# Four changes to the order of VectorE's work in the attention of a convolution block

## The chip, the cores and the metric

The kernel runs on one core of one Trainium2 chip. The metric is device time in microseconds from start to end of one execution, as the median of several runs. The profile is of one execution, taken by the hardware profiler. Engines are named as the profile names them: PE is TensorE, DVE is VectorE, ACT is ScalarE, POOL is GpSimd, SP is SyncE, which only issues transfers here.

## The reference

The input is x with 8 images of 512 channels and 32x32 pixels, all in fp32. The block normalises it in groups of 16 channels, runs a block of convolutions with attention on it, and adds x:

```python
t = cbs(x, cv1_w, cv1_bn, 0)                      # 1x1, 512 -> 512, batch norm, silu
ys = [t[:, :C], t[:, C:]]                         # C = 256
for i in range(N):                                # N = 2 bottlenecks
    yi = ys[-1]
    z = cbs(yi, m_cv1_w[i], m_cv1_bn[i], 1)       # 3x3, 256 -> 256
    z = bot_attention(z, m_qkv_w[i], m_rw[i], m_rh[i])
    z = jax.nn.silu(bn_eval(conv2d(z, m_cv2_w[i], 0), m_cv2_bn[i]))
    ys.append(yi + z)
return cbs(jnp.concatenate(ys, axis=1), cv2_w, cv2_bn, 0)   # 1x1, 1024 -> 512
```

The attention has 4 heads of 64 channels over the 1024 pixels:

```python
logits = jnp.einsum('bhdi,bhdj->bhij', q, k + r) * HD ** (-0.5)   # r = rw + rh
a = jax.nn.softmax(logits, axis=-1)
out = jnp.einsum('bhij,bhdj->bhdi', a, v)
```

The outermost step is `x + block(_gn(x))`.

## The kernel before

The images follow each other, and each goes through: 3x3 convolution of the first bottleneck (a Winograd form: `tiles_in` makes the inputs on VectorE, `conv3x3` multiplies, `columns_out` and `rows_out` put the outputs together), its projection to q, k and v, its attention, its 1x1 convolution `m2`, then the same for the second bottleneck, then the last 1x1 convolution. The first 1x1 convolution of the next image (`cv1`) lies at the end of the first bottleneck's attention, which is why the next image's group norm is computed during that attention.

The instructions of each engine run in the order in which they were put into that engine's queue. The order is set by hand with `tc.issue_after(ins)`: what is written under it gets its place behind `ins`. A tile from a pool with `bufs=n` waits until the tile that had the same place n allocations before has been read. The page's `L` numbers are lines of the kernel before.

**Projection.** Image 1 uses `project`, and images 2 to 8 use `project_strassen`, which multiplies 2x2 blocks with seven products instead of eight, and needs more sums on VectorE. Its last five operations finish the second half of the pixels (`half` 1) for the first 128 channels (`c` 0): k1 += u (L626), add_r(0, 1), which adds rw (L577) and rh (L578) to k1, v1 += u (L628) and q1 += u (L629). The sums for the second 128 channels' r are put off to `later()`.

**Attention** (`attention_fast`). There are four groups g: two blocks of 128 channels (two heads each) times two halves of 512 query pixels. A group has eight blocks j of 128 key pixels, taken in pairs. So an attention has 16 pairs, and i counts them. For each pair:

- `logits(pair)`: TensorE makes the logits of two heads by 512 queries for each j (L662, eight matmuls, which the trace shows as 16 records), in a PSUM tile `l_ps` of the pool `ps_big` (3 tiles of two banks). ScalarE takes Exp of it into `pt` (L666). VectorE adds the `pt` into `acc`: the first pair of a group by one sum of its two halves (L672), later pairs by two sums (L674).
- `times_v(previous pair)`: TensorE multiplies the previous pair's `pt` by v into `av_ps` (L688). There is one `av_ps` tile (`ps_av`, bufs=1), two banks, for a whole group. After the last pair of a group it is evicted: ScalarE copies the first bank to `ao` (L695), VectorE adds the second (L696). The next group's first product waits for that.

TensorE is therefore one pair ahead with logits: at a group change it does the new group's first two pairs of logits, the old group's sums of Exp, and then the new group's first product.

**Divisions.** `sums(g)` adds `acc` over partitions with matmuls (`s_ps`, L706). ScalarE copies the row, and it goes through DRAM to be spread over partitions, is inverted by `spread(g)` (L750), goes to DRAM again and comes back as `rs`, broadcast over the partitions. `scale(g, rs)` multiplies `ao` by it (L762). `spread(g - 1)` is placed at the third pair of group g, and `scale(g - 2)` at the first pair.

**Work behind attention.** `behind` maps a group, or a group and a pair, to a function that is called there. In the first bottleneck `ahead` is called in each of the four groups. It takes one step of the next image's group norm with `next(norm)`: statistics of two channel blocks (L443), statistics of the other two, the mean over groups of channels (a matmul `gm_ps`, L449, in a `ps_big` tile, and small sums on VectorE), then deviation and the normalising of x (L477). The first group takes none, groups 1, 2 and 3 take one each, and one more is taken in the third pair of group 2. In image 1, `ahead` also makes 3x3 weights for the second bottleneck (`make`, tiles `u_new`) on VectorE.

Of the kernel before, what the change touches and what calls it, by code (L numbers as in the profile page):

```python
# [47 lines left out]
ALU = mybir.AluOpType  # L48
# [13 lines left out]
def kernel(  # L62
# [16 lines left out]
    nc = tc.nc  # L79
# [33 lines left out]
    def load_w1():  # L113
        w = ring([P, NX, 2 * C], "w1")
        nc.sync.dma_start(w, cv1_w.rearrange("(k p) o -> p k o", p=P))
        return w
# [189 lines left out]
    def load_u(n, oc, i):  # L306
        u = new_u("u")
        nc.sync.dma_start(u, u_dram[n][oc][i])
        return u
# [7 lines left out]
    def img(ap):  # L317
        return ap.rearrange("p (h w) -> p h w", w=F)

    def inner(yp, c, half):  # L320
        return yp[:, c, 1 + half * ROWS : 1 + (half + 1) * ROWS, :].rearrange("p h w -> p (h w)")

    def stages(act, small, ps_big, ps_av, n_pt):
# [6 lines left out]
        def table_of(func):  # L330

            nc.scalar.activation(spare, zero, func)
# [204 lines left out]
        def project_strassen(n, z, sq, mid):  # L537
# [6 lines left out]
            tt = nc.vector.tensor_tensor  # L544
# [25 lines left out]
            def v_of(ap):  # L570
                return ap.rearrange("p (j o) -> p j o", o=P)

            def add_r(c, half, src=None):
                dst = img(kr[:, c, ts(half, HALF)])
                rw = rw_sb[:, n, c, :].unsqueeze(1).to_broadcast([P, ROWS, F])
                rh = rh_sb[:, n, c, ts(half, ROWS)].unsqueeze(2).to_broadcast([P, ROWS, F])
                tt(dst, dst if src is None else img(src), rw, ALU.add)  # L577
                tt(dst, dst, rh, ALU.add)  # L578

            t = act.tile([P, 4, HALF], F32, tag="pt", name="t_z", bufs=n_pt)  # L580
            t1, t2, t3, t4 = (t[:, i] for i in range(4))
# [40 lines left out]
            with tc.issue_after(freed.ins):  # L622
                tt(v3, v2, v_of(m5[:, 2]), ALU.add)
                last = tt(v2, v2, v_of(ps_v[:, 0]), ALU.subtract)
            with tc.issue_after(last.ins):
                tt(k1, k1, u[:, 1], ALU.add)  # L626
                add_r(0, 1)
                tt(v1, v1, v_of(u[:, 2]), ALU.add)  # L628
                tt(q1, q1, u[:, 0], ALU.add)  # L629

# [6 lines left out]
        def attention_fast(n, z, at, behind, sq=None, mid=None):  # L637
# [3 lines left out]
            q, kr, vT, later = (*project(n, z), None) if sq is None else project_strassen(n, z, sq, mid)  # L641
# [6 lines left out]
            pairs = [steps[i : i + PAIR] for i in range(0, len(steps), PAIR)]  # L648
            pts, accs, avs = {}, {}, {}

            def logits(pair):
                g, j0 = pair[0]
                c, half = groups[g]
                pt = act.tile([P, PAIR, 2, HALF], F32, tag="pt", name="pt", bufs=n_pt)
                pts[pair[0]] = pt
                for i, (_, j) in enumerate(pair):
                    ps = ps_big.tile([P, 2, HALF], F32, tag="big", name="l_ps")
                    for hd in range(2):
                        r = slice(hd * HD, (hd + 1) * HD)
                        for kh in range(2):  # L660
                            o = j * P + kh * HD
                            nc.tensor.matmul(  # L662
                                ps[kh * HD : (kh + 1) * HD, hd, :], kr[r, c, o : o + HD],
                                q[r, c, ts(half, HALF)], start=True, stop=True,
                            )
                    exp = nc.scalar.activation(pt[:, i], ps, AF.Exp, scale=SCALE)  # L666
                if pair is pairs[-1]:
                    with tc.issue_after(exp.ins):
                        table_of(AF.Silu)
                if j0 == 0:  # L670
                    accs[g] = act.tile([P, 2, HALF], F32, tag="acc", name="acc", bufs=2)
                    return nc.vector.tensor_tensor(accs[g], pt[:, 0], pt[:, 1], ALU.add)  # L672
                for i in range(PAIR):
                    ins = nc.vector.tensor_tensor(accs[g], accs[g], pt[:, i], ALU.add)  # L674
                return ins

            def times_v(pair):
                g, j0 = pair[0]
                c, half = groups[g]
                pt = pts.pop(pair[0])  # L680
                if j0 == 0:
                    avs[g] = ps_av.tile([P, 2, HALF], F32, tag="av", name="av_ps")
                for i, (_, j) in enumerate(pair):
                    for kh in range(2):
                        r = slice(kh * HD, (kh + 1) * HD)
                        for hd in range(2):
                            o = c * P + hd * HD
                            nc.tensor.matmul(  # L688
                                avs[g][hd * HD : (hd + 1) * HD, kh, :], vT[r, j, o : o + HD],
                                pt[r, i, hd, :], start=(j == 0), stop=(j == NJ - 1),  # L690
                            )
                if j0 + PAIR == NJ:
                    av = avs.pop(g)
                    dst = ao[:, c, ts(half, HALF)]
                    nc.scalar.copy(dst, av[:, 0])  # L695
                    nc.vector.tensor_tensor(dst, av[:, 1], dst, ALU.add)  # L696

            def sums(g):

# [46 lines left out]
            def spread(g, s_dram):  # L746

                rs = act.tile([P, HALF], F32, tag="rs", name="rs", bufs=2)
                rc = small.tile([P, QP], F32, tag="rc", name="rc", bufs=2)
                nc.vector.reciprocal(rc, total(g, s_dram))  # L750
                r_dram = tc.dram_tile([2, HALF], F32, name=f"r_dram{at + g}")
                nc.sync.dma_start(r_dram.rearrange("h (i r) -> (h i) r", r=QP), rc)
                for hd in range(2):
                    nc.sync.dma_start(
                        rs[hd * HD : (hd + 1) * HD, :], r_dram[hd : hd + 1, :].to_broadcast([HD, HALF])
                    )
                return rs

            def scale(g, rs):
                c, half = groups[g]  # L760
                dst = ao[:, c, ts(half, HALF)]
                nc.vector.tensor_tensor(dst, dst, rs, ALU.mult)  # L762
# [2 lines left out]


            NQ = NJ // PAIR
            s_drams, rss = {}, {}
            for i in range(len(pairs) + 1):
                if i < len(pairs):  # L770
                    added = logits(pairs[i])
                    g, at_q = divmod(i, NQ)
                    with tc.issue_after(added.ins):
                        if at_q == NQ - 2 and g > 0:
                            rss[g - 1] = spread(g - 1, s_drams[g - 1])
                        if i == 1 and later is not None:
                            later()
                        if at_q == 0 and g > 1:
                            scale(g - 2, rss.pop(g - 2))
                if i > 0:  # L780
                    g, j0 = pairs[i - 1][0]
                    if j0 == 0 and g > 0:
                        s_drams[g - 1] = sums(g - 1)
                    times_v(pairs[i - 1])
                    with tc.issue_after(added.ins):
                        behind.get(g if j0 == 0 else (g, j0 // PAIR), lambda: None)()
            with tc.issue_after(added.ins):
# [2 lines left out]
            g = len(groups) - 1  # L790
# [319 lines left out]
    with tc.issue_after(made.ins):  # L1110
# [4 lines left out]
        for at in bn_m1:  # L1115
            last = nc.vector.tensor_scalar(sh[:, at : at + NM], sh[:, at : at + NM], -1 / 12, None, ALU.mult)
# [5 lines left out]
    last = made  # L1122
# [6 lines left out]
    for b in range(B):  # L1129
# [41 lines left out]
        norm = s.group_norm(xs) if more else iter(())  # L1171
        groups = iter(range(NM * NH))

        def ahead():
            nonlocal w1
            g = next(groups)
            if g > 0:
                next(norm, None)
            if g == 0:
                w1 = load_w1() if more else load_w2(1)  # L1180
                if b > 0:
                    for at in ((0, 0), (0, 1), (0, 2), (1, 0)):
                        us[at] = load_u(1, *at)
            if b == 0:
                if g == 0:
                    raws[1, 1, 0], raws[1, 1, 1] = load_raws_y0(1, 1)
                    make(1, 1, [2])
                    del us[1, 2]
                elif g <= NM:
                    make(1, 1, [0], [g - 1])  # L1190
# [14 lines left out]

        NG = NM * NH
        behind = {g: ahead for g in range(NG)} | {NG: first, NG + 1: second}
        behind[NG - 2, 2] = lambda: next(norm, None)
        if b == 0:
            behind[-1] = lambda: make(1, 0, range(PAIRS))  # L1210
        ao, check = s.attention_fast(0, z, b * N * NM * NH, behind, sq.get(0), mid)
        last = s.m2(0, ao, y1, lambda oc, half: inner(y2, oc, half))
# [44 lines left out]
        behind = {1: ahead, NG: first, NG + 1: second}  # L1257
# [4 lines left out]
        last = s.m2(1, ao, y2, lambda oc, half: ylast[:, oc, ts(half, HALF)])  # L1262
# [27 lines left out]
    with tc.If(held < P):  # L1290
        with ExitStack() as gs:
# [6 lines left out]
            g = stages(g_act, g_small, g_big, g_av, 3)  # L1298
# [67 lines left out]
```

## Time and profile before

The median of three runs is 2366.81 us (2366.19 to 2371.23).

| what | before |
|---|---|
| span of the profiled execution | 2365.4 us |
| mean granted TensorE clock | 0.997 |
| VectorE, sums of Exp (L674 and L672) | 469.5 and 78.3 us |
| VectorE, division (L762) x64 | 44.1 us busy, 65.8 us idle before it |
| VectorE, eviction (L696) x64 | 43.8 us |
| TensorE, product with v (L688) and logits (L662) | 487.8 and 486.1 us |
| chain of waits, TensorE | 89% of the span |

A group's busy time is the union of its instructions' times; "idle before" is the time in which that engine stood still just ahead of such an instruction, with what ended it. The arrow in a timeline line, such as `[0.15 <-DVE ao L696]`, says the same for one instruction. In the timeline neighbours of the same kind are merged, and x16 counts them.

### The profile page before, as it was taken

The page shows a single profiled execution, that of the slowest core. Times are in us where ns is not written, and L with a number is a line of the kernel's source. Part 1 is how long each engine was busy: PE and PEld are TensorE (multiplying, and loading weights), DVE is VectorE, ACT ScalarE, POOL GpSimd, SP SyncE. Part 2 cuts the span into 40 slices and gives each one's busy share as a digit, 9 for nine tenths or more (in the row PEclk, how much of TensorE's full clock was granted, in tenths as well). Part 3 has the DMA queues.
Part 4 walks back from the last instruction along what each step waited for, and adds up shares of the span by engine and source line. Part 5 has one row for each costly group of instructions (what it writes and reads, how often), then busy time and mean ns, then how long its engine had stood idle before and what let it go on. Part 6 is the DMA issues. An engine that isn't in the chain of part 4 may idle for free.

```text
span 2365.4 us, 36291 instructions
## 1 busy us (share of the span) xinstructions
PE 2321.6 (98%) x14794; PEld 1181.0 (50%) x14794; DVE 1751.7 (74%) x2811; ACT 944.5 (40%) x1246; POOL 87.9 (4%) x305
## 2 busy tenths in 40 slices
PE   7999999999999999999999999999999999999998
PEld 4536346363553635536364463645536364463643
DVE  8866777677786877868678675886767867677674
ACT  1442524435244351544425344253433525335352
POOL 1000000000100001000010000100001000000001
PEclk9999999999999999999999999999999999999999
DMA  7412225030340304303052031611207021160202
GB/s 251 152 53 89 91 90 213 16 129 15 123 176 15 130 15 164 140 10 130 23 208 89 29 112 33 248 42 54 86 28 263 29 85 55 42 221 15 85 10 69
DMA packets 93069, 226.39 MB, mean 96 GB/s; under 512 B 27872, under 2 KB 49312, under 8 KB 80224
## 3 DMA queue, kind: packets, MB, share of 16 engines
q1 hardware_dynamic: 81376, 174.71, 21.8%
q0 software_dynamic: 11520, 49.29, 5.3%
q8 instruction: 118, 1.93, 0.3%
q14 instruction: 55, 0.45, 0.1%
HBM read 190.41 MB, written 33.55 MB: 95 GB/s over the span
## 4 chain that ended last, share of the span: by engine, by line
PE 89%; DVE 6%; DMA 2%; ACT 2%; issue 1%; SPq 0%; POOL 0%; DVEq 0%; ACTq 0%
PE av_ps L688 16%; PE l_ps L662 15%; PE c_ps L879 14%; PE ps L343 12%; PE c L934 8%; PE p_ps L556 7%; PE c_new L934 6%; PE m_ps L900 5%; PE pv_ps L560 3%; DVE acc L674 2%; ACT pt L666 1%; PE p_ps L560 1%; DVE acc L672 1%; PE s_ps L724 1%; DMA rs<-r_dram 1%; PE s_ps L706 1%
## 5 line engine op out<-in xcount | busy, mean ns | idle before, releaser
L666 ACT ACTIVATE pt<-l_ps 128x1024 f32<-128x1024 f32 x512 | 494.9, 1023 | 425.0 <-PE l_ps L662 423.6
L674 DVE TENSOR_TENSOR acc<-acc,pt 128x1024 f32<-128x1024 f32 x384 | 469.5, 1223 | 84.9 <-ACT pt L666 60.1
L688 PE MATMUL av_ps<-pt,vT 64*64 64x512 f32 x4096 | 487.8, 593 | 10.7 <-DVE ao L696 10.7
L662 PE MATMUL l_ps<-q,kr 64*64 64x512 f32 x4096 | 486.1, 591 | 0.9
L879 PEld LDWEIGHTS c_ps<-v_in,u 128*128 128x128 f32 x2720 | 306.3, 192 | 7.9 <-issue 6.7
L879 PE MATMUL c_ps<-v_in,u 128*128 128x128 f32 x2720 | 306.9, 275 | 1.1 <-DVE v_in L400 1.1
L688 PEld LDWEIGHTS av_ps<-pt,vT 64*64 64x64 f32 x4096 | 157.1, 133 | 284.0 <-issue 216.7
L662 PEld LDWEIGHTS l_ps<-q,kr 64*64 64x64 f32 x4096 | 158.2, 133 | 269.6 <-issue 255.4
L343 PE MATMUL ps<-x,w 128*128 128x512 f32 x512 | 227.1, 600 | 2.2 <-DVE x L477 2.2
L343 PEld LDWEIGHTS ps<-x,w 128*128 128x128 f32 x512 | 97.0, 192 | 130.3 <-issue 127.2
L407 ACT COPY m<-c_ps 128x256 f32<-128x256 f32 x96 | 35.4, 369 | 224.9 <-PE c_ps L879 219.8
L934 PE MATMUL c_new<-t_in,ws 128*128 128x512 f32 x288 | 124.6, 592 | 0.0
L672 DVE TENSOR_TENSOR acc<-pt 128x1024 f32<-128x1024 f32 x64 | 78.3, 1223 | 58.0 <-ACT pt L666 58.0
L900 PE MATMUL m_ps<-ao,m_sb 128*128 128x512 f32 x256 | 112.5, 592 | 0.0
L762 DVE TENSOR_TENSOR ao<-ao,rs 128x512 f32<-128x512 f32 x64 | 44.1, 689 | 65.8 <-DMA rs<-r_dram 65.1
L328 ACT ACTIVATE m_kept<-m_kept,bh,sh 128x512 f32<-128x512 f32 x42 | 31.9, 806 | 146.0 <-DVE m_kept L1018 86.3
L934 PEld LDWEIGHTS c_new<-t_in,ws 128*128 128x128 f32 x288 | 54.8, 190 | 68.8 <-issue 66.0
L328 ACT ACTIVATE t<-m_ps,bh,sh 128x512 f32<-128x512 f32 x64 | 48.0, 775 | 83.9 <-PE m_ps L900 82.5
L556 PE MATMUL p_ps<-t_z,sq 128*128 128x512 f32 x168 | 81.3, 593 | 0.0
L372 POOL MEMSET w_rows<- 128x16 f32 x96 | 12.2, 127 | 1805.6 <-PE s_ps L706 1111.8
L900 PEld LDWEIGHTS m_ps<-ao,m_sb 128*128 128x128 f32 x256 | 48.7, 190 | 61.2 <-issue 61.2
L328 ACT ACTIVATE z<-z,bh,sh 128x512 f32<-128x512 f32 x64 | 48.6, 806 | 50.9 <-DVE z L436 50.9
(223 smaller groups left out, 2704.9 us busy)
## 6 DMA issues: line engine op xcount, KB each, us to landing
u<-u SPq DMA_DIRECT2D x85, 1024.0 KB
x<-in_x_dram SPq DMA_DIRECT2D x32, 512.0 KB
x_res<-in_x_dram POOLq DMA_DIRECT2D x28, 512.0 KB, 8.1
out_dram<-m_kept POOLq DMA_DIRECT2D x28, 512.0 KB, 7.5
w<-in_cv_w_dram SPq DMA_DIRECT2D x13, 1024.0 KB
u<-u_new POOLq DMA_DIRECT2D x12, 1024.0 KB, 5.8
rs<-r_dram SPq DMA_DIRECT2D x96, 128.0 KB
ws<-s SPq DMA_DIRECT2D x24, 512.0 KB
```

Source lines behind the costliest of these rows:

```text
L328: return nc.scalar.activation(dst, src, AF.Silu, scale=sh[:, k : k + 1], bias=bh[:, k : k + 1])
L343: nc.tensor.matmul(ps[:, half, :], w_of(k), rhs_of(k, half), start=(k == begin), stop=(k == end))
L556: nc.tensor.matmul(ps[:, o, :], w[:, o, :], rhs, start=not onto, stop=True, skip_group_check=onto)
L560: nc.tensor.matmul(v[:, ts(j, P)], rhs[:, ts(j, P)], w[:, 2, :], start=j == 0 and not onto, stop=True, skip_group_check=True,)
L662: nc.tensor.matmul(ps[kh * HD : (kh + 1) * HD, hd, :], kr[r, c, o : o + HD], q[r, c, ts(half, HALF)], start=True, stop=True,)
L666: exp = nc.scalar.activation(pt[:, i], ps, AF.Exp, scale=SCALE)
L672: return nc.vector.tensor_tensor(accs[g], pt[:, 0], pt[:, 1], ALU.add)
L674: ins = nc.vector.tensor_tensor(accs[g], accs[g], pt[:, i], ALU.add)
L688: nc.tensor.matmul(avs[g][hd * HD : (hd + 1) * HD, kh, :], vT[r, j, o : o + HD], pt[r, i, hd, :], start=(j == 0), stop=(j == NJ - 1),)
L879: nc.tensor.matmul(ps[:, row, col, :], us[i][:, k, row, SLOT[col], :], vs[i][:, k, row, col, :], start=(k == 0), stop=(k == NM - 1),)
L900: nc.tensor.matmul(pss[oc][:, half, :], m2_sb[:, n, k, ts(oc, P)], ao[:, k, ts(half, HALF)], start=(k == 0), stop=(k == NM - 1),)
L934: nc.tensor.matmul(ps[:, o, :], w[:, k, ts(o, P)], rhs[part][:, c, :], start=(k == 0 and not onto), stop=(k == KB - 1), skip_group_check=onto,
```

## The change

The change reorders four pieces of VectorE's work. No arithmetic is added or removed.

1. In `project_strassen`, the three operations that finish k are put ahead of those of v and q, since the logits read k first.
2. In attention with `later` (images 2 to 8), at the first group change the eviction of `av_ps` is put ahead of the new group's first sum, which moves into a function `add_up`.
3. `scale(g - 2)` moves from the first pair of a group to the second, so behind the eviction that frees the bank.
4. In image 1, the norm of the second image starts one group earlier: `ahead` takes a step in group 0 too, and the additional step in group 2 is left out there.

```diff
-                tt(dst, dst, rh, ALU.add)
+                return tt(dst, dst, rh, ALU.add)
...
             with tc.issue_after(last.ins):
                 tt(k1, k1, u[:, 1], ALU.add)
-                add_r(0, 1)
+                last = add_r(0, 1)
+            with tc.issue_after(last.ins):
                 tt(v1, v1, v_of(u[:, 2]), ALU.add)
                 tt(q1, q1, u[:, 0], ALU.add)
...
+                if j0 == 0 and g == 1 and later is not None:
+                    accs[g] = None
+                    return exp
+                return add_up(pair)
+
+            def add_up(pair):
+                g, j0 = pair[0]
+                pt = pts[pair[0]]
                 if j0 == 0:
                     accs[g] = act.tile([P, 2, HALF], F32, tag="acc", name="acc", bufs=2)
                     return nc.vector.tensor_tensor(accs[g], pt[:, 0], pt[:, 1], ALU.add)
...
-                    nc.vector.tensor_tensor(dst, av[:, 1], dst, ALU.add)
+                    evicted[0] = nc.vector.tensor_tensor(dst, av[:, 1], dst, ALU.add)
...
-                        if at_q == 0 and g > 1:
+                        if at_q == 1 and g > 1:
                             scale(g - 2, rss.pop(g - 2))
...
                     times_v(pairs[i - 1])
+                    if i < len(pairs) and accs.get(pairs[i][0][0], 0) is None:
+                        with tc.issue_after(evicted[0].ins):
+                            added = add_up(pairs[i])
...
-            if g > 0:
+            if g > 0 or b == 0:
                 next(norm, None)
...
-        behind[NG - 2, 2] = lambda: next(norm, None)
-        if b == 0:
+        if b > 0:
+            behind[NG - 2, 2] = lambda: next(norm, None)
+        else:
             behind[-1] = lambda: make(1, 0, range(PAIRS))
```

In the order of the instructions on each engine, the queues of ScalarE, GpSimd and SyncE are as before. On TensorE only the second image's `gm_ps` moves, from behind the third product of group 2 to behind the first. The rest is on VectorE. In images 2 to 8 the five operations L626, L628, L577, L629 and L578 run k, v, k, q, k before, and k, k, k, v, q afterwards.

More of the change, by code (lines that the diff above doesn't have):

```diff
@@ L767, in attention_fast @@
             NQ = NJ // PAIR
-            s_drams, rss = {}, {}
+            s_drams, rss, evicted = {}, {}, [None]
             for i in range(len(pairs) + 1):
```

## The prediction

> **What bounds the kernel now.** I read the page's first part, then the list of TensorE's waits, then the timeline around attention, where every edit lies.
>
> ```profile
> PE 2321.6 (98%) x14794; PEld 1181.0 (50%) x14794; DVE 1751.7 (74%) x2811; ACT 944.5 (40%) x1246; POOL 87.9 (4%) x305
> PE av_ps L688 <- DVE ao L696: 10.7, 20, 3.9
> ```
>
> TensorE (PE) is busy for 98% of the span, so only its gaps can be won. The second line says that the first product with v of a group (av_ps) waited 20 times for VectorE's second half of the eviction (ao, L696), 10.7 us in all, once 3.9 us. These idle times start only when the last record has drained, so they understate the loss. A better measure is the step from the start of one run of 16 matmul records to the start of the next, taken from the timeline. In attention, a run of logits (l) or of product with v (a) takes a step of 1.72 us, the four sums matmuls (S) 0.57 us. The next lines are one steady attention (image 2, second bottleneck), at its start and at its first and second group change.
>
> ```profile
> 533.55 0.69 DVE L578 TENSOR_TENSOR kr<-kr,rh_sb 128x512 f32<-128x512 f32 x1
> 534.15 1.22 DVE L672 TENSOR_TENSOR acc<-pt 128x1024 f32<-128x1024 f32 x1
> 534.38 1.95 PE L662 MATMUL l_ps<-q,kr 64*64 64x512 f32 x16
> 536.12 1.93 PE L688 MATMUL av_ps<-pt,vT 64*64 64x512 f32 x16
> ...
> 544.97 0.59 ACT L695 COPY ao<-av_ps 128x512 f32<-128x512 f32 x1 [0.64 <-PE av_ps L688]
> 545.48 1.22 DVE L672 TENSOR_TENSOR acc<-pt 128x1024 f32<-128x1024 f32 x1
> 546.56 0.64 PE L706 MATMUL s_ps<-acc,ones 128*32 128x256 f32 x8
> 546.62 0.69 DVE L696 TENSOR_TENSOR ao<-av_ps,ao 128x512 f32<-128x512 f32 x1
> 547.36 1.95 PE L688 MATMUL av_ps<-pt,vT 64*64 64x512 f32 x16 [0.15 <-DVE ao L696]
> ...
> 560.81 0.68 DVE L696 TENSOR_TENSOR ao<-av_ps,ao 128x512 f32<-128x512 f32 x1
> 561.25 0.64 PE L706 MATMUL s_ps<-acc,ones 128*32 128x256 f32 x8
> 561.82 1.95 PE L688 MATMUL av_ps<-pt,vT 64*64 64x512 f32 x16
> ```
>
> First stop: the third run of logits is the first to read the second half of k. VectorE ends that half at 534.24 and the run starts at 534.38. The step from the av_ps run at 532.43 is 1.95 us instead of 1.72. Second stop: at the first group change VectorE does the first sum of the new group (L672) ahead of the eviction that frees the bank; S takes 0.80 us instead of the 0.57 of the second change (561.25 to 561.82). All 14 attentions of images 2 to 8 have both stops, 1.95 or 1.96 and 0.79 or 0.80.
>
> The first image's first attention is the worst. It takes 62.35 us from its first logits to its last product, where the other seven first bottlenecks take 55.21 to 56.76.
>
> ```profile
> 124.80 1.22 DVE L672 TENSOR_TENSOR acc<-pt 128x1024 f32<-128x1024 f32 x1
> 127.32 0.69 DVE L762 TENSOR_TENSOR ao<-ao,rs 128x512 f32<-128x512 f32 x1 [1.30 <-DMA rs<-r_dram]
> 127.93 0.68 DVE L696 TENSOR_TENSOR ao<-av_ps,ao 128x512 f32<-128x512 f32 x1
> 128.67 1.95 PE L688 MATMUL av_ps<-pt,vT 64*64 64x512 f32 x16 [1.86 <-DVE ao L696]
> ...
> 146.54 0.69 DVE L762 TENSOR_TENSOR ao<-ao,rs 128x512 f32<-128x512 f32 x1 [3.38 <-DMA rs<-r_dram]
> 147.15 0.68 DVE L696 TENSOR_TENSOR ao<-av_ps,ao 128x512 f32<-128x512 f32 x1
> 147.89 3.39 PE L688 MATMUL av_ps<-pt,vT 64*64 64x512 f32 x16 [3.89 <-DVE ao L696]
> ```
>
> The reader is to see the order on VectorE: the division of the group before the last (L762) waits for its reciprocals from DRAM, the eviction stands behind it, and TensorE waits for the eviction. S takes 2.50 and 4.53 us here. The last line also lasts 3.39 us instead of 1.9: the clock was down.
>
> [...] The trace has 685 to 692 and 1223, so I use the trace. [...] L578, which reads what L577 wrote, starts 0.72 us after it (519.07 to 519.79), while neighbours that don't depend on each other start 0.60 us apart (533.55 to 534.15). I take 0.12 us for each dependent pair. [...] after the 3.89 us stop the window from 148 to 151 us shows a clock of 0.52.
>
> **Part 1, k ahead of v and q.** Now the five operations that finish the second half run k, v, k, q, k (L626, L628, L577, L629, L578), then L672. Afterwards the three of k follow each other, then v and q. From L626 at 531.14: 531.86, 532.58, end 533.27, which is 0.97 us earlier than 534.24 and well before 534.15, where TensorE wants it. The stop goes: step 1.95 to 1.72, with 0.02 to 0.03 more from the steps behind it, 0.26 us. Times 14: 3.6 us. The price is two dependent pairs, so VectorE is 0.24 us later from L672 on. Who waits for that? v and q are done by about 534.5, and are first read by the product at 539.6 and the logits at 541.3. The sums matmul waits for the old group's last sum, which ends at 545.57 and then at 545.81; TensorE, 0.26 us earlier, comes to it at 546.3. About 0.45 us are left.
>
> **Part 2, the bank of the product with v.** In these 14 attentions the eviction goes ahead of L672 at the first group change. It can start when ScalarE's copy is there (545.56, now earlier) and the sum before it is out of the way (545.48 + 0.24): 545.72, end 546.4. TensorE wants the bank at 546.3 + 0.57 = 546.83. S falls from 0.80 to 0.57 and the run ahead of it from 1.86 to 1.83: 0.25 us, times 14: 3.5 us. Behind the moved sum stand only sums, which wait for Exp anyway.
>
> **Part 3, divisions.** L762 goes from the first to the second pair of a group, behind eviction and sums, with 3.4 us more for its DMA. Its 0.69 us is not new work. In second bottlenecks it fits into VectorE's idle time there (1.61 us before the sums at 565.75). In first bottlenecks it only trades places with the eviction. Three late arrivals in images 3 and 6 go (S of 1.45, 1.24 and 1.39 to 0.57): 0.88 + 0.67 + 0.82 = 2.4 us. In the first image S 2.50 and 4.53 would fall to 0.57, which is 1.9 + 4.0 us, the slow clock goes (3.32 to 1.88, 1.4 us), and so does a late PSUM slot behind gm_ps (step 1.99 to 1.72, 0.3 us): 7.6 us.
>
> **Part 4, statistics of the second image.** One step of the norm moves one group earlier. The matmul gm_ps moves by four runs and costs the same 0.32 us. VectorE gets four BATCH_NORM_STATS2 and two aggregates in group 0, 2.45 us (114.52 to 116.97), so that group 2 has less. The new image's x was asked for at 41 to 47 us, so it has landed by 101. VectorE had 0.99 us idle before the first sum of group 1; 1.4 us are left over, and there the eviction still stands behind that sum. It ends at 112.86 instead of 111.44, and TensorE waits until 112.91 instead of 112.28: 0.6 us lost. At the next change VectorE's shifted row ends the eviction at 127.36 and TensorE wants it at 127.37: even. gm_ps holds a PSUM slot until its copy at about 132.0, which is wanted at 133.0. So the first image brings 7.6 - 0.6 = 7.0 us: 55.3 us for that attention, like the others.
>
> **Sum.** 3.6 + 3.5 + 2.4 + 7.0 = 16.5 us. No other wait takes it back: between the attentions the chain of waits is unbroken TensorE (c_ps 21.44, ps or c 13.73 us in each image), and no TensorE wait names a DMA. So 2366.8 - 16.5 = 2350.3 us.
>
> **Rivals.** (a) The first image's load of VectorE is the true bound. Groups 0 to 2 hold statistics and the making of weights (u_new), and the sum of VectorE's work there is unchanged; if the early statistics push sums and evictions back at each change and the slow clock returns, half of the 7.0 goes: 2353.8. For it speaks that VectorE has no idle time from 112 to 126 us; against it, that 1.30 and 3.38 us of the stops are pure DMA waits. (b) Parts 1 and 2 give nothing: VectorE is behind all through the first group, and its 0.24 us turn up at the sums matmul. Then only 2.4 + 7.0 remain: 2357.4. Against it are the 0.4 us of room at both places. (c) Slower: the divisions still wait for DMA, now with sums behind them, and those hold up the next S; the 0.24 us show in 14 attentions (3.4) and the statistics cost 2.45 in group 0, with no stop removed: 2366.8 + 5.9 = 2372.7. For it speaks only that the DMA was up to 4.9 us late for L762; against it, that S for that group comes 10 us later.
>
> **How the numbers follow.** My forecast 0.68, (a) 0.14, (b) 0.11, (c) 0.03, something unseen 0.04. The late DMAs of images 3 and 6 differ from run to run, worth 2.4 us either way, and the first image is known to about 2 us. Hence 2346 to 2358, which takes in (a) and (b). Faster 0.94 (forecast, a, b and a little of the unseen), same 0.03, slower 0.03.
>
> **What would show it.** In the changed profile: steps of 1.72 us in the third run of logits; S of 0.57 at all three changes in images 2 to 8; no L696 directly behind an L762; S near 1.2 at the first change of image 1; no slow clock near 148 us; a first attention of 55 to 56 us. I would be wrong if S stayed at 0.8, with the old group's sum as its releaser, or if L762's waits came back as waits of s_ps or x.

## The result and the profile after

The changed kernel takes 2349.52 us (median of 6 runs, 2348.76 to 2350.84). The kernel before, run with it, takes 2368.48 us (2366.19 to 2371.23). The ratio is 0.992, with a 95% interval of 0.9907 to 0.9933. The prediction was 2350.3 us, a gain of 16.5 us; the medians differ by 19.0 us.

Lines of the kernel have moved: the first sum of a group is now L681 (it was L672), the later sums L683 (L674), the product with v L697 (L688), the two halves of its eviction L704 and L705 (L695, L696), the sums matmul L715 (L706), the division L771 (L762).

First the page's line of busy times of the changed kernel:

```profile
PE 2314.2 (99%) x14794; PEld 1169.5 (50%) x14794; DVE 1757.3 (75%) x2811; ACT 944.9 (40%) x1246; POOL 88.2 (4%) x305
```

Then its list of TensorE's waits (total us, times, longest us):

```profile
PE av_ps L697 <- DVE ao L705: 1.1, 2, 0.6
PE c L946 <- DVE ao L705: 0.6, 1, 0.6
```

Of the 20 waits of the product with v for the eviction, 10.7 us in all, two are left, and both are in image 1. The second line is a wait that the list of the kernel before doesn't have; it comes up again below. The number of instructions on each engine is as before.

Next lines from the timeline of the second bottleneck of image 2, at the same places as in the prediction:

```profile
523.55 0.69 DVE L578 TENSOR_TENSOR kr<-kr,rh_sb 128x512 f32<-128x512 f32 x1
525.11 1.90 PE L663 MATMUL l_ps<-q,kr 64*64 64x512 f32 x16
...
531.57 5.21 DVE L683 TENSOR_TENSOR acc<-acc,pt 128x1024 f32<-128x1024 f32 x4
536.70 0.68 DVE L705 TENSOR_TENSOR ao<-av_ps,ao 128x512 f32<-128x512 f32 x1
537.23 0.64 PE L715 MATMUL s_ps<-acc,ones 128*32 128x256 f32 x8
537.80 1.95 PE L697 MATMUL av_ps<-pt,vT 64*64 64x512 f32 x16
```

The reader is to see two things. The k row ends at 524.24, well ahead of the third run of logits at 525.11, which now follows the run before it (523.39) by 1.72 us. And the eviction (L705) starts as the old group's sums end, and is over at 537.38, 0.42 us ahead of the product that needs the bank. S, the step from the sums matmuls (537.23) to that product (537.80), is 0.57 us.

And the first attention of image 1, at its second and third group change:

```profile
123.34 1.22 DVE L681 TENSOR_TENSOR acc<-pt 128x1024 f32<-128x1024 f32 x1
124.47 0.68 DVE L705 TENSOR_TENSOR ao<-av_ps,ao 128x512 f32<-128x512 f32 x1
124.62 0.64 PE L715 MATMUL s_ps<-acc,ones 128*32 128x256 f32 x8
125.21 1.95 PE L697 MATMUL av_ps<-pt,vT 64*64 64x512 f32 x16
127.54 0.69 DVE L771 TENSOR_TENSOR ao<-ao,rs 128x512 f32<-128x512 f32 x1
...
138.62 0.69 DVE L705 TENSOR_TENSOR ao<-av_ps,ao 128x512 f32<-128x512 f32 x1
139.58 0.64 PE L715 MATMUL s_ps<-acc,ones 128*32 128x256 f32 x8
140.15 1.95 PE L697 MATMUL av_ps<-pt,vT 64*64 64x512 f32 x16
142.39 0.69 DVE L771 TENSOR_TENSOR ao<-ao,rs 128x512 f32<-128x512 f32 x1
```

The divisions (L771) come behind the product that they held up before, and these two wait for no DMA any more: neither line has a bracket. S is 0.59 and 0.57 us, where it was 2.50 and 4.53. The clock from 146 to 149 us is 1.00. Over all 64 divisions the waiting for DMA has fallen only from 65.1 to 55.5 us: 7.6 us of what has gone are the five waits that stood ahead of an eviction at a group change.

Where the time came from, by the steps between runs of matmuls, from the first logits of each attention to the start of its last two runs of products, which the timeline merges into one line (to the start of the very last run it is 1.72 us more, before and after):

| TensorE time, us | before | after | predicted gain | gain |
|---|---|---|---|---|
| first attention of image 1 | 62.35 | 55.27 | 7.0 | 7.1 |
| second attention of image 1 | 54.44 | 54.44 | 0 | 0.0 |
| the other 14 | 767.69 | 758.08 | 3.6 + 3.5 + 2.4 = 9.5 | 9.6 |
| sum | 884.48 | 867.79 | 16.5 | 16.7 |

The spans of the two profiles differ by 18.4 us. Besides the 16.7 us, 2.1 us lie ahead of the first attention, which begins at 94.4 and 92.3 us, with the same instructions. There TensorE waits twice for weights (1.3 and 1.2 us), and in the profile before the clock is 0.50 for 3.4 us just after that (65.5 to 68.9 us), where it stays at 1.00 in the profile after: a run of 52 matmul records takes 7.70 us there and 6.07 us here. This has nothing to do with the change. It comes and goes between profiles of one kernel (the changed kernel has it in one of its two, with 6.07 and 7.69 us for that run), and is worth 1.6 us; it is the noise to keep in mind below, and the steps don't have it.

On the other side, 0.7 us are lost behind the second attention of image 1. There, at 292.19 us, the division of the last group but one waits 4.60 us for its reciprocals; last sum and last eviction stand behind it, and the last 1x1 convolution (`c`, L946) waits 0.60 us for the eviction, the second line of the list above. The end of the program is 0.3 us shorter. This stop, too, comes and goes: it costs 0.4 to 0.8 us in six of the ten profiles that have part 3 (in the changed kernel, one of two), and nothing in the four that don't.

### The profile page after: what moved, and what is told of

It is laid out like the page before. It is cut to its first block, busy times and chain, and to the rows that moved or that the text cites. A ratio compares the mean times of both kernels' runs of the same rounds, so it can differ in the third digit from the quotient of the medians.

```text
span 2347.0 us, 36305 instructions
## 1 busy us (share of the span) xinstructions
PE 2314.2 (99%) x14794; PEld 1169.5 (50%) x14794; DVE 1757.3 (75%) x2811; ACT 944.9 (40%) x1246; POOL 88.2 (4%) x305
## 4 chain that ended last, share of the span: by engine, by line
PE 94%; DVE 4%; DMA 1%; ACT 0%; issue 0%; POOL 0%; SPq 0%; DVEq 0%; ACTq 0%
PE av_ps L697 18%; PE l_ps L663 18%; PE c_ps L891 14%; PE ps L343 12%; PE c L946 8%; PE p_ps L556 7%; PE c_new L946 6%; PE m_ps L912 5%; PE pv_ps L560 3%; PE s_ps L715 1%; PE p_ps L560 1%; PE s_ps L733 1%; DVE acc L683 1%; PE v_ps L527 1%; DMA x_res<-in_x_dram 0%
## 5 line engine op out<-in xcount | busy, mean ns | idle before, releaser
L683 DVE TENSOR_TENSOR acc<-acc,pt 128x1024 f32<-128x1024 f32 x384 | 469.6, 1223 | 84.4 <-ACT pt L667 60.7
L697 PE MATMUL av_ps<-pt,vT 64*64 64x512 f32 x4096 | 485.1, 591 | 1.1 <-DVE ao L705 1.1
L697 PEld LDWEIGHTS av_ps<-pt,vT 64*64 64x64 f32 x4096 | 152.0, 133 | 277.3 <-issue 235.6
L946 PE MATMUL c_new<-t_in,ws 128*128 128x512 f32 x288 | 124.6, 592 | 0.0
L681 DVE TENSOR_TENSOR acc<-pt 128x1024 f32<-128x1024 f32 x64 | 78.2, 1221 | 48.3 <-ACT pt L667 48.3
L946 PEld LDWEIGHTS c_new<-t_in,ws 128*128 128x128 f32 x288 | 54.7, 190 | 68.9 <-issue 66.0
L771 DVE TENSOR_TENSOR ao<-ao,rs 128x512 f32<-128x512 f32 x64 | 44.1, 689 | 56.1 <-DMA rs<-r_dram 55.5
L920 DVE TENSOR_TENSOR ylast<-t,ypad 128x512 f32<-128x512 f32 x32 | 22.0, 693 | 63.9 <-ACT t L328 63.9
```

Of the source, the lines that this page charges most:

```text
L697: nc.tensor.matmul(avs[g][hd * HD : (hd + 1) * HD, kh, :], vT[r, j, o : o + HD], pt[r, i, hd, :], start=(j == 0), stop=(j == NJ - 1),)
L946: nc.tensor.matmul(ps[:, o, :], w[:, k, ts(o, P)], rhs[part][:, c, :], start=(k == 0 and not onto), stop=(k == KB - 1), skip_group_check=onto,
```

## The experiments

The theory was that of the prediction: each stop of TensorE is a queue on VectorE, and moving the waited-for instruction ahead removes it. The rivals were that parts stand or fall alone, that VectorE's idle quarter hides anything, and that the first image is held up by VectorE's work, not by its order. Each run is given with its median time and its ratio to the kernel before with the 95% interval, and then with what the steps show. A "first bottleneck" takes 55.21 us and a "second bottleneck" 54.26 us in the kernel before, where no DMA is late; 54.69 and 53.74 in the changed one. (Image 8's first bottleneck has no next image to normalise, and takes what a second one does; the prediction's range of 55.21 to 56.76 for the other first bottlenecks leaves it out.)

### Each part alone

Part 1 alone, on the kernel before:

```diff
...
-                add_r(0, 1)
+                last = add_r(0, 1)
+            with tc.issue_after(last.ins):
                 tt(v1, v1, v_of(u[:, 2]), ALU.add)
```

> Part 1 alone on the kernel before. My theory: not additive. The third run of logits no longer waits (step before it 1.95 to 1.72 us, 14 times), but VectorE is 0.24 us later at the first group change and the eviction still stands behind the new group's first sum, so that S grows from 0.80 to about 1.34 us. Net +0.25 us in each of 14 attentions: about 3.5 us slower than before, near 2372. Rival (each part is worth its own sum): 3.6 us faster, near 2365. Second rival (VectorE has idle time, 0.24 us hide): 3.6 us faster with S still at 0.80.

2369.95 us, ratio 1.0009 (1.0000 to 1.0017). The stop at the third logits is gone (1.72), and S is 1.32 or 1.33 in the 14 attentions. Second bottlenecks take 54.50 us instead of 54.26. The timeline of this kernel, image 2, second bottleneck (its lines: first sum L673, eviction L696 and L697, sums matmul L707, product L689):

```profile
545.41 0.58 ACT L696 COPY ao<-av_ps 128x512 f32<-128x512 f32 x1 [0.63 <-PE av_ps L689]
546.44 1.22 DVE L673 TENSOR_TENSOR acc<-pt 128x1024 f32<-128x1024 f32 x1
546.99 0.64 PE L707 MATMUL s_ps<-acc,ones 128*32 128x256 f32 x8
547.57 0.68 DVE L697 TENSOR_TENSOR ao<-av_ps,ao 128x512 f32<-128x512 f32 x1
548.31 1.95 PE L689 MATMUL av_ps<-pt,vT 64*64 64x512 f32 x16 [0.68 <-DVE ao L697]
```

ScalarE's half of the eviction is over at 545.99, but VectorE does the new group's sum first, and the eviction ends at 548.25. TensorE, which came earlier, waits longer: it gains 0.26 us at the first stop and loses 0.5 us at the second. So part 1 alone is not worth 3.6 us. It is worth a little less than nothing, as the theory of a common queue says; the rival of parts that add up is refuted, and so is the one in which 0.24 us hide. The loss in time, 1.95 us, is less than the 3.5 that was expected, and a time alone can't tell them apart here: the late divisions of images 3, 6 and 7 cost 1.5 us in this profile where they cost 2.4 in the one before, and the first attention, which the edit doesn't touch, takes 64.3 us instead of 62.35. The changed kernel without part 2, below, has part 1 without late divisions: its 14 attentions take 3.6 us more than those of part 3 alone.

Part 2 alone:

```diff
+                if j0 == 0 and g == 1 and later is not None:
+                    accs[g] = None
+                    return exp
...
                     times_v(pairs[i - 1])
+                    if i < len(pairs) and accs.get(pairs[i][0][0], 0) is None:
+                        with tc.issue_after(evicted[0].ins):
+                            added = add_up(pairs[i])
```

> Part 2 alone on the kernel before. My theory: S at the first change of images 2 to 8 falls from 0.80 to 0.57 us, step of the third logits stays at 1.95: 14 times 0.25 us, 3.5 us faster, near 2365. Rival (the eviction then waits for ScalarE's copy or for the old group's last sum instead): S between 0.65 and 0.80, under 2 us faster.

2366.19 us, ratio 0.9991 (0.9984 to 0.9997). S is 0.57 at all 14 first changes, the third logits still stop (1.95), and second bottlenecks take 54.02 us: 0.24 us less, which would be 3.4 us for 14. The 14 attentions together fell by 2.8 us, and the median by 1.8. Part of the gain comes back at the next changes, where the divisions still stand ahead of the eviction: this profile has ten late divisions in place of five. Four of the new ones, in the first bottlenecks of images 4, 5 and 7, bring S at the second change to 0.85, 0.84 and 0.73 and at the third, in image 7, to 0.83. The first two of these attentions gain nothing. Why there are more of them here was not followed. And the clock is halved four times near or in image 1 (at 65, 130, 150 and 225 us; mean granted clock 0.996), where the profile before has two such windows (0.50 from 65.5 and from 147.5 us, 3.4 us each; mean 0.997). Whether that is the whole difference in all runs isn't settled.

Part 3 alone:

```diff
-                        if at_q == 0 and g > 1:
+                        if at_q == 1 and g > 1:
                             scale(g - 2, rss.pop(g - 2))
```

> Part 3 alone. My theory: nearly all of the first image's gain is here, with or without the early statistics: S of 2.50 and 4.53 us both near 0.6, no slow clock at 148 us, and late arrivals in later images no longer show: 9 to 10 us faster, near 2359, of which 7.3 in the first attention (62.35 to about 55.0). S at the first changes of images 2 to 8 stays at 0.80. Rival (the early statistics are what makes room in group 2): S stays above 1.5 at one of the two changes and the first attention takes over 58 us.

2359.75 us, ratio 0.9962 (0.9949 to 0.9976): 8.25 us, a little less than the 9 to 10 expected. The first attention takes 55.29 us, all but 0.02 us of what the four parts together bring there, and first and second bottlenecks of later images take 55.20 and 54.25, none with a late division. The four profiles without part 3 have 5, 5, 10 and 5 late divisions at group changes, the ten with it none. The rival, that the early statistics are needed, falls. The timeline of the first attention (lines as in the kernel before):

```profile
124.02 1.22 DVE L672 TENSOR_TENSOR acc<-pt 128x1024 f32<-128x1024 f32 x1
125.15 0.68 DVE L696 TENSOR_TENSOR ao<-av_ps,ao 128x512 f32<-128x512 f32 x1
125.40 0.64 PE L706 MATMUL s_ps<-acc,ones 128*32 128x256 f32 x8
125.97 1.95 PE L688 MATMUL av_ps<-pt,vT 64*64 64x512 f32 x16
...
138.84 0.15 DVE L452 COPY gm<-gm_ps 128x4 f32<-128x4 f32 x1
139.06 1.95 PE L662 MATMUL l_ps<-q,kr 64*64 64x512 f32 x16 [0.36 <-DVE gm L452]
```

The upper lines show an eviction that comes in time without the early statistics. The lower two show what part 4 is good for: the small tile gm_ps sits in a PSUM slot until VectorE copies it, and logits wait for that slot, a step of 2.26 us instead of 1.72. In the kernel before it was 1.99, so part 3 alone makes this stop longer.

Part 4 alone:

```diff
-            if g > 0:
+            if g > 0 or b == 0:
                 next(norm, None)
...
-        behind[NG - 2, 2] = lambda: next(norm, None)
-        if b == 0:
+        if b > 0:
+            behind[NG - 2, 2] = lambda: next(norm, None)
+        else:
```

> Part 4 alone. My theory: S at the first change of image 1 grows from 0.57 to 1.13 us, S at the second stays near 2.5 (the reciprocals start 0.7 us later, and so do the matmuls), S at the third falls, since the reciprocals are asked for 1.5 to 2 us earlier: between 1 and 3 instead of 4.53, and the slow clock may go. 1 to 5 us faster. Rival (statistics only cost VectorE time): 0.5 us slower or no change.

2363.31 us, ratio 0.9979 (0.9971 to 0.9987). S in the first attention is 1.13, 2.73 and 0.57 us, and it takes 59.02 us. As expected, with the work moved out of group 2 the division at the third change is no longer late; S was expected between 1 and 3 us there, and there is no wait at all. The second wait stays:

```profile
127.29 0.69 DVE L762 TENSOR_TENSOR ao<-ao,rs 128x512 f32<-128x512 f32 x1 [1.46 <-DMA rs<-r_dram]
127.90 0.68 DVE L696 TENSOR_TENSOR ao<-av_ps,ao 128x512 f32<-128x512 f32 x1
128.64 3.35 PE L688 MATMUL av_ps<-pt,vT 64*64 64x512 f32 x16 [2.09 <-DVE ao L696]
```

The product behind that wait takes 3.35 us instead of 1.95, as in the kernel before where the clock was 0.50 (3.39 us, at 147.89), though TensorE had stood still for 2.09 us only. In the kernel before, the same stop of 1.86 us was not followed by a slow run (1.95 us, clock 1.00 from 128.5 to 131 us); in part 2 alone one of 2.04 us was.

### One part less

The changed kernel without part 4 (its edits undone):

> The changed kernel without part 4. My theory: with the divisions out of the way the early statistics cost more than they bring: S at the first change of image 1 goes from 1.13 to 0.57 (-0.56 us), the late PSUM slot behind gm_ps comes back (+0.27 us): 0.3 us faster than the changed kernel, first attention 55.0 us. Rival (part 4 makes the room that part 3 needs): S above 1.5 at the second or third change, over 2 us slower than the changed kernel.

2351.83 us, ratio 0.993 (0.9917 to 0.9944). The first attention takes 55.30 us against 55.27. S at the first change is 0.57 as expected, but the slot behind gm_ps costs 0.55 us (step 2.27), not 0.27, so the two cancel. The rival falls too. In the presence of part 3, part 4 is worth nothing that can be told.

The changed kernel without part 2:

> The changed kernel without part 2. My theory: the eviction stands behind a sum that is itself 0.24 us later while TensorE is 0.26 us earlier: S 1.34 us at the first change of images 2 to 8, so 0.77 us lost 14 times: 10.8 us slower than the changed kernel, near 2360. Rival (parts are additive): 3.5 us slower, near 2353.

2361.34 us, ratio 0.9974 (0.9963 to 0.9984). S is 1.33 or 1.34 at the first change of all 14 attentions, and these take 768.78 us instead of 758.08: 10.7 us, more than three times what part 2 brings alone. Parts 1 and 2 are one change: together they bring 7.2 us, part 2 alone at most 3.4, part 1 alone a loss.

### Where in the group the division stands

The divisions of groups 0 and 1 go back to the first pair, but directly behind the eviction:

```diff
-                        if at_q == 1 and g > 1:
-                            scale(g - 2, rss.pop(g - 2))
...
+                    if j0 + PAIR == NJ and g > 0 and g < 3:
+                        with tc.issue_after(evicted[0].ins):
+                            scale(g - 1, rss.pop(g - 1))
```

> The changed kernel with the divisions of groups 0 and 1 back at the first pair, but directly behind the eviction. Theory A (being behind the eviction is what counts): S stays at 0.57 to 0.6 at all changes of images 2 to 8, the DMA waits of L771 stand in front of sums that have room: 0 to 2 us slower than the changed kernel, all of it in image 1. Theory B (the 3.4 us more for the DMA count as much): waits come back at the sums or at the statistics, over 4 us slower.

2350.77 us, ratio 0.9928 (0.9914 to 0.9941). The first attention takes 55.81 us, 0.54 more, all of it at the slot behind gm_ps (step 2.22), whose copy on VectorE is late. All later attentions take 54.69 or 54.70 and 53.74. So it is the place behind the eviction that counts. The 3.4 us more that the DMA gets are worth half a microsecond in the first attention of image 1, and in this profile 1.3 us more just behind it: VectorE comes late to the next reciprocals, the attention's last sum ends late, and the sums matmul (L733, at 162.08) waits 1.26 us for it, where it doesn't wait in the changed kernel. Together this is within the 0 to 2 us of theory A.

### How much room VectorE has

One more operation behind the last one of q, in each of the 14 attentions:

```diff
                 tt(q1, q1, u[:, 0], ALU.add)
+                tt(q1, q1, q1, ALU.max)
```

> The changed kernel with one more VectorE operation behind the last one of q (q1 = max(q1, q1), which changes no value), 0.60 to 0.72 us in each of 14 attentions. My theory: VectorE has 0.37 us of room before the first group change, measured from the end of the eviction to the matmul that waits for it; what goes beyond shows: 0.23 to 0.35 us each, 3 to 5 us slower than the changed kernel. Rival (VectorE is idle for 25% of the span, so one more operation is free): no change.

2351.26 us, ratio 0.9928 (0.9915 to 0.9942). The step ahead of S is 1.92 instead of 1.83, nothing else changes, and the attentions take 54.78 and 53.83 us: 0.09 us more each. One of the 14 attentions is an exception: in the first bottleneck of image 4 the step is 2.27, after a pause of VectorE of 0.46 us at 969.4 us whose cause was not found.

And with two:

```diff
                 tt(q1, q1, u[:, 0], ALU.add)
+                tt(q1, q1, q1, ALU.max)
+                tt(q1, q1, q1, ALU.max)
```

> The same with two such operations, 1.1 to 1.4 us in each of 14 attentions (they are placed between the first sums). My theory: 0.37 us of room, the rest shows: 0.7 to 1.05 us each, 10 to 15 us slower than the changed kernel. Rival (free): no change. Rival (VectorE is simply in series): all of it shows, 15 to 20 us slower.

2355.84 us, ratio 0.9947 (0.9933 to 0.996). The step ahead of S is 2.32 or 2.33, and the attentions take 55.20 and 54.25: 0.5 us more each, 7.0 us for 14. The timeline of image 2, second bottleneck (sums L685, eviction L707, sums matmul L717):

```profile
532.95 5.20 DVE L685 TENSOR_TENSOR acc<-acc,pt 128x1024 f32<-128x1024 f32 x4
538.07 0.68 DVE L707 TENSOR_TENSOR ao<-av_ps,ao 128x512 f32<-128x512 f32 x1
538.30 0.64 PE L717 MATMUL s_ps<-acc,ones 128*32 128x256 f32 x8 [0.42 <-DVE acc L685]
```

The wait is at the sums matmul, for the old group's last sum, which ends at 538.15; the matmul starts 0.15 us later. From the first operation to the second the cost grows by 0.40 us, and the first costs 0.09. So, taking both operations to cost the same, one is worth 0.40 us here, and the room is 0.31 us. The changed kernel's own timeline says the same: the old group's last sum ends at 536.78, the sums matmul starts at 537.23, and of these 0.45 us 0.15 are the time from the sum's end to the matmul's start, as measured with two operations (538.15 to 538.30). Both expectations were too high, since they took 0.60 us or more for an operation. These operations stand between sums that depend on each other (526.21 between 525.08 and 526.82 in the run with one of them), and part of their time was a pause before: the first sum and the next started 1.32 us apart, and with the operation between them 1.74. That VectorE is idle for a quarter of the span makes nothing free here: the room is a third of a microsecond.

### Further than the change

The eviction ahead of the new group's first sum in image 1 too:

```diff
-                if j0 == 0 and g == 1 and later is not None:
+                if j0 == 0 and g == 1:
```

> The changed kernel with the eviction ahead of the new group's first sum in image 1 too. My theory: S of 1.13 and 1.26 us at the first changes of image 1's two attentions fall to 0.57: 1.25 us faster than the changed kernel. Rival: the load of statistics and weights on VectorE holds up the old group's last sum, and S stays above 0.8 in the first attention: under 0.8 us faster.

2349.35 us, ratio 0.9923 (0.991 to 0.9937). The second attention takes 53.74 us, 0.70 less, as expected. In the first one S at the first change falls from 1.13 to 0.57, but at the second it rises from 0.59 to 1.35, and the attention takes 55.47 us. There the rival was right in kind, though one change later: VectorE has no pause of more than 0.11 us from 100 to 126 us, and TensorE only came earlier to wait for it.

Both of this and no part 4:

> The changed kernel without part 4 and with the eviction first in image 1 too. With the early statistics gone, VectorE comes to the second change of the first attention in time, so S is 0.57 at all changes of both attentions of image 1 (1.35 at the second change with the early statistics); the late PSUM slot behind gm_ps stays (0.5 us). First attention 55.3, second 53.7: 0.7 us less TensorE time than the changed kernel, less than a time alone can tell. Rival: S above 0.7 at a change of image 1 again, and then no gain.

2350.99 us, ratio 0.9933 (0.992 to 0.9947). The second attention again takes 53.74 us, but the first takes 55.92: S at the second change is 1.13 here too. The timeline tells why:

```profile
110.70 0.69 DVE L705 TENSOR_TENSOR ao<-av_ps,ao 128x512 f32<-128x512 f32 x1 [2.22 <-ACT ao L704]
...
125.38 1.22 DVE L681 TENSOR_TENSOR acc<-pt 128x1024 f32<-128x1024 f32 x1
126.52 0.68 DVE L705 TENSOR_TENSOR ao<-av_ps,ao 128x512 f32<-128x512 f32 x1
127.26 1.95 PE L697 MATMUL av_ps<-pt,vT 64*64 64x512 f32 x16 [0.49 <-DVE ao L705]
```

Without the early statistics VectorE is done with the old group early, and with the eviction first it now stands still for 2.22 us until ScalarE's copy is there, where it did the new group's sum before. That time is missing one group later. So the version that was to beat the changed kernel doesn't. The lower lines show that the wait at the second change is a matter of order again: the new group's first sum (125.38) stands ahead of the eviction, as it did at the first change. Started in its place, the eviction would end at about 126.06, and TensorE, whose sums matmuls start at 126.13, wants the bank at 126.13 + 0.57 = 126.70; this is an estimate from this profile. A version with the eviction first at the second change too was not run.

The changed kernel again, on the same chip as this last version:

> The changed kernel once more, on the same chip as the last version, to compare the two directly: first attention 55.3, second 54.4, and 0.7 us slower than that version by the steps; the clock windows of 3.4 us near 64 us decide up to 1.7 us of either.

2350.21 us, ratio 0.9928 (0.9915 to 0.9942), with the first two attentions at 55.26 and 54.44. The last version and the changed one can't be told apart by time, and the sums of their 16 attentions are 867.74 and 867.77 us.

## Why the prediction was right, step by step

- **What bounds the kernel: right.** In attention the gain is TensorE's stops; the sum of the steps fell by 16.7 us where 16.5 were predicted. "No other wait takes it back" does not quite hold: the stop of 0.60 us behind image 1's second attention does in some profiles, though it names VectorE, as a division waits for DMA ahead of the eviction.
- **Part 1, k ahead: right inside the whole change** (step 1.72), **wrong as a sum of its own.** The prediction gave it 3.6 us, "TensorE, 0.26 us earlier, comes to it at 546.3", and asked only whether the sums matmul had room. Alone it loses, since with the eviction still behind the new sum TensorE's 0.26 us turn into waiting and VectorE's 0.24 us are added to that.
- **Part 2, the bank: right** (S 0.57 in all 14, worth 3.4 us where no division is late). Undone in the changed kernel it costs 10.7 us. The two figures don't contradict each other: 3.4 us, and 14 times the 0.24 us of VectorE and the 0.26 us of TensorE that part 1 brings, are 10.4.
- **Room at the sums matmul: mis-sized.** "About 0.45 us are left" is the right distance from the sum's end to the matmul's start, but the room is 0.31: in the run with two operations, where the matmul waited for that sum, it started 0.15 us after the sum's end (538.15 and 538.30). It was enough.
- **Part 3, divisions: right in its main terms**, with S at 0.59 and 0.57, the slow clock gone and no late arrival left at a group change. Its 0.3 us for the PSUM slot had the wrong sign: with part 3 alone that step grows from 1.99 to 2.26, and the first attention gains 7.1 us where 7.6 were given to part 3. That the place behind the eviction counts, and not the time for the DMA, was not separated in the prediction; the runs did that.
- **Part 4, statistics: its cost right** (S 1.13 at the first change where 1.2 was expected, 0.59 at the second), its worth not worked out. Without it the first attention takes the same time: 0.56 us at the first change pay for 0.55 us at the PSUM slot. So the predicted 7.0 us of parts 3 and 4 came out at 7.1 partly by luck: what part 3 was given too much is what part 4 was given too little.
- **The slow clock: right** in that it goes with the stop (0.50 from 147.5 to 150.9 us before, 1.00 from 146 to 149 us after). **Not foreseen:** the 2.1 us ahead of the first attention, 1.6 of them a slow clock that one profile had (0.50 from 65.5 to 68.9 us) and the other not.
- **The number: closer than the working deserves.** The gain of the medians is 19.0 us and not 16.5; the time came within 0.8 us of the prediction since the kernel before took 1.7 us more in six runs than in the three it was predicted from. In a later comparison the medians differ by 17.4 us (2367.64 and 2350.21). Where the medians part from the steps isn't settled: two profiles can't tell, and without part 3 the first attention alone takes 62.35 to 64.3 us from profile to profile (leaving out part 4 alone, which has 59.02).
- **Rival (a)** was not what happened to the change. It is nearer to what met the two versions that free TensorE earlier in image 1: their first attention takes 55.47 and 55.92 us, no less than 55.3, since TensorE then waits for VectorE at the second change. Whether VectorE's load is the bound there, or once more its order, was not tested; the lines at 125.38 and 126.52 us above speak for the order.

## What to carry to other kernels

An engine with a quarter of its time idle can still be the bound of a stretch (VectorE, busy for 75% of the span, had 0.31 us of room at the first group change): look at what stands ahead of the instruction that the bound engine waits for, and put it first. Don't price edits to one queue one by one: an edit that lets the waiting engine come earlier is worth nothing while the next wait on the same queue stands (part 1 alone a loss, parts 1 and 2 together 7.2 us). And an early place for a releasing instruction has a price where it makes its own engine wait for something else, as the eviction did for ScalarE's copy (2.22 us).

## What the runs showed of the hardware

Short stops of TensorE were followed by half clock in some places and not in others. After the stop of 2.09 us (part 4 alone) the product's 16 records took 3.35 us instead of 1.95, and after one of 2.04 us (part 2 alone) the clock was halved too; after those of 1.86 us (kernel before, clock 1.00 from 128.5 to 131 us) and 1.91 us (part 1 alone) it was not. Two stops of 1.3 and 1.2 us near 63 us were followed by it in 11 of 14 profiles (mean granted clock 0.996 to 0.998, and 0.999 in the other three): in the kernel before it was 0.50 from 65.5 to 68.9 us. A single stop of 1.2 us, at 214 to 224 us, was followed by it in 2 of 14; in the one with the divisions directly behind the eviction the 8 records after it took 5.40 us, where they took 3.70 in the kernel before. What decides between them was not shown.

On VectorE one fp32 TENSOR_TENSOR of 128x512 took 685 to 692 ns in the kernel before (means of L696 and L400) and one of 128x1024 1223 ns (L672 and L674); the prediction reckons with these. An operation put between two VectorE sums that depend on each other cost 0.40 us (the step ahead of S was 1.92 us with one and 2.32 with two), where independent neighbours of that size start 0.60 us apart (523.88 and 524.48 in the run with one operation). In the run with two such operations a matmul started 0.15 us after the end of the sum that it waited for (538.15 and 538.30).
